# A graph-attention layer with residual and row norm on one core: two blocks leave the table of x rows, and three small pieces of work change places

## The chip, the cores and the metric

The kernel runs on one core of a Trainium2 chip. Its time is device time in microseconds (us). Before the change it takes 233.98 us, the median of three runs (233.9 to 234.27). The profile is of one execution of its own, which took 233.53 us; its span, from the first to the last instruction of the program, is 232.0 us, and the times inside it are counted from its start. The granted TensorE clock is 0.98 of full speed over that execution.

## The reference, cut to what matters

```python
def _L0_gnn_ref(h, adj_mat, W, a):          # h: 4096 x 512, adj: 4096 x 4096, W: 512 x (4*512)
    ht = (h @ W).reshape(N, 4, 512).transpose(1, 0, 2)
    src = jnp.einsum('hnd,hd->hn', ht, a[:, :512, 0])
    dst = jnp.einsum('hnd,hd->hn', ht, a[:, 512:, 0])
    e = jax.nn.leaky_relu(src[:, :, None] + dst[:, None, :], 0.01) + adj_mat[None]
    att = jax.nn.softmax(e, axis=-1)
    return jnp.einsum('hij,hjd->hid', att, ht).mean(axis=0)

x = _layernorm(x + _L0_gnn_ref(x, adj, W, a), axis=-1)
```

The entries of `adj` reach 1e9, and the largest of a row stands far above the second. The softmax then is 1 at that column and 0 elsewhere, so a row of the result is the row of x at the column of the row's maximum, times the mean of W over the heads, plus the row's own x, normalised. The kernel computes that for all rows, tests on the chip that the largest entry leads by enough (with a bound from the norms of x, W and a), and has a general path for inputs where it does not; with these inputs that path is not taken.

## The kernel before, in words

The 4096 rows are worked in 32 blocks of 128 rows, one row on each partition. One Python loop over steps t = 0 to 31 writes the instructions out, in the order in which each engine will run them; nothing is reordered later. A block passes through several steps, so that in one step different engines work on different blocks:

- SP issues the load of block t + 5 of adj (`load_adj`, L128; 2 MB; six buffers) and of x in groups. The general order on its queue is that of the loop; the stores come last.
- VectorE takes maxima over segments of block t (`segment_maxima`, L212), finds the segment with the largest (`find_segment`, L222 and L224), and, two blocks later, the place inside it (`find_column`, L264 and L270). The last block is searched over its whole row (`find_column_in_row`, L278).
- GpSimd gathers the segment that has the maximum (the leads, L230) and then the rows of x at the columns found (`gather_rows`, L250 or L255), with one indirect DMA each for 128 rows.
- TensorE turns the gathered rows of block t - 3 (`turn`: four transposes, L284), adds the block's own x by a product with the identity (`residual`, L296) and multiplies by the mean of W (`products`, L303, four times). ScalarE copies the turned rows (L286), sums squares (L347), and takes mean and variance (L372, L374).
- Blocks from 24 on (`BEHIND`) are handled differently: 24 to 27 are put by (`put_by`, L353), get their x added on GpSimd, and are normalised at the end (`stats`, `late_factors`, `finish`, L366, L368, L391); 28 to 30 get their moments on VectorE (L411, L415), a root on ScalarE (L417), and the normalisation on VectorE (L427). Block 31 is worked in two halves of its columns (L400, L434, L440).

**The table.** `TABLED` lists blocks in which columns below 128 are not gathered. The product of the first 128 rows of x with the mean of W stands in three bf16 parts z. For such a block GpSimd moves those columns out of bounds, so that the gather skips them, ScalarE clears the buffer beforehand (`clear_rows`, L245), `spread` (L331, L333, L335) makes a 0/1 matrix of the columns below 128 and `from_table` (L343) multiplies it with the three parts. In a block that is not in the list the gather fetches all 128 rows; there is no clearing, no spread and no product with z.

**Norms of heads.** `head_norms` has three parts, one a step: `each` on VectorE (L473) and two small products on TensorE (L475, L476); sums on VectorE (L480, L484) and a root on ScalarE (L485); the sum and maximum on VectorE (L488, L489). The result is used only at the end, in `bound` (L507).

Of the kernel before, what the change touches and what calls it, by code (L numbers as in the profile page):

```python
# [26 lines left out]
EARLY = 18  # L27
LAST = 4
SKIP = 8192
TABLED = range(1, 28)  # L30


@with_exitstack
# [40 lines left out]
def leading_rows(ctx, tc, x, adj, W, a, out, ident, leads, any_bad):  # L74
# [11 lines left out]
    KB, NB = D // P, N // P  # L86
# [4 lines left out]
    LATE = NB - Q  # L91
# [200 lines left out]
    def residual(ib):  # L292
        start = ib not in o_ps
        if start:
            o_ps[ib] = psum.tile([P, D], F32, name="o")
        nc.tensor.matmul(o_ps[ib], ident, hold[:, ib, :], start=start, stop=False)  # L296
# [172 lines left out]
    def head_norms(part):  # L469

        if part == 0:
            each = once.tile([2 * H, 2 * H], F32, name="each")
            nc.vector.tensor_scalar_mul(each, ident[: 2 * H, : 2 * H], aa)  # L473
            pw = of_norms[0] = psum.tile([P, KB * H + 2 * H], F32, name="o")
            nc.tensor.matmul(pw[:, : KB * H], ones, ww, start=True, stop=True)  # L475
            nc.tensor.matmul(pw[:, KB * H :], ones[: 2 * H, :], each, start=True, stop=True)  # L476
        elif part == 1:
            pw = of_norms[0]
            w2 = once.tile([P, H], F32, name="w2")
            nc.vector.tensor_reduce(  # L480
                w2, pw[:, : KB * H].rearrange("p (k h) -> p h k", h=H), axis=AX.X, op=OP.add
            )
            for s in range(2):
                nc.vector.tensor_mul(n2[:, ts(s, H)], pw[:, ds(KB * H + s * H, H)], w2)  # L484
            nc.scalar.activation(n2, n2, AF.Sqrt)  # L485
        else:
            both = once.tile([P, H], F32, name="both")
            nc.vector.tensor_add(both, n2[:, :H], n2[:, H:])  # L488
            nc.vector.tensor_reduce(vn, both, axis=AX.X, op=OP.max)  # L489
# [56 lines left out]
    for t in range(NB):  # L546
        if t == NB // 2:
            tc.mark_branch_hint_location("general", engines=HINTED)
        if t in x_at:
            load_x(*x_at[t])  # L550
        if t + AHEAD == NB - 1:
            load_x(LATE, 2)
        load_adj(t + AHEAD)
        middle = PIECES if t in END else 1 if t == NB - 1 else 2
        segment_maxima(t, 0, middle)
        if t >= COLUMN and t not in END and t != COLUMN + 1:
            find_column(t - COLUMN)
            if t == lag_of(BEHIND) + 1:
                scales(slice(BEHIND - 2, BEHIND))
        if t not in END:  # L560
            segment_maxima(t, middle, PIECES)
        if t == NB - 1:
            for ib in (BEHIND, LATE + 2, BEHIND + 2):
                load_x(ib, 2)
        find_segment(t)
        if t in END:
            find_column(t - 1 if t <= COLUMN else t - COLUMN)
        if t + 1 in TABLED:
            clear_rows(t + 1)
        for lo, hi in FACTORS:  # L570
            if t == lag_of(hi):
                nc.vector.reciprocal(sd[:, lo:hi], sd[:, lo:hi])
                if hi < BEHIND:
                    scales(slice(lo, hi))
        if t < 2:
            mean_of_heads(t)
        elif t == 2:
            mean_of_heads(2)
            mean_of_heads(3)
            fill_table()  # L580
        if t == 0:
            square_sums_of_a()
        if 21 <= t < 24:
            head_norms(t - 21)
        ib = t - PROJECT
        if t == NB - 2:
            finish(BEHIND - 3)
            finish(BEHIND - 2)
        if t == NB - 1:
            row_norm(LATE)  # L590
            row_norm(LATE + 1)
            finish(BEHIND - 1)
            residual(LATE + 1)
        if ib >= 0:
            if ib in TABLED:
                spread(ib)
            turn(ib)
            if ib > BEHIND:
                products(ib - 1, KB - 1, KB)
            if ib < BEHIND:  # L600
                residual(ib)
            if ib in TABLED:
                from_table(ib)
            products(ib, 0, KB if ib < BEHIND else KB - 1)
            if ib == 0:
                split_table()
        for _ in range(squares_at.get(t, 0)):
            square_sum_of_w(squares.pop(0))
        if t >= BEHIND + STATS:
            put_by(t - STATS)  # L610
        elif t >= STATS:
            row_norm(t - STATS)
            parked_stats(t - STATS)
        for lo, hi in FACTORS:
            if t == hi - 1 + STATS:
                root(slice(lo, hi))
        for done in FINISHED.get(t, ()):
            finish(done)
# [51 lines left out]
    products_of_half(NB - 1, 0)  # L670
    products_of_half(NB - 1, 1)
    add_sums(NB - 2, hold[:, NB - 2, :])
    moments(NB - 2)
    finish(BEHIND + 2)
    stats_of_half(NB - 1, 0)
    factor(NB - 2)
    normalise(NB - 2, o_ps.pop(NB - 2))
    finish(LATE - 1)
    stats_of_half(NB - 1, 1)
    moments(NB - 1)  # L680
    factor(NB - 1, shift=True)
# [190 lines left out]
```

## Time and profile before

| what | value |
|---|---|
| median of three runs | 233.98 us (233.9 to 234.27) |
| the profiled execution | 233.53 us, span 232.0 us |
| adj loads | 38 issues, 28 of them 2 MB each, landing in a median of 33.1 us |
| gathers of rows of x | 32, median 8.3 us from issue to landing |
| HBM traffic | 418 GB/s over the span |

A row of the page's groups reads: line, engine, operation, what it writes and reads, its count, then the busy time, the mean of one in ns, and the idle time just before it with what ended that. A row of a timeline reads: start in us, duration in us, engine, line, operation, and in square brackets how long the engine was idle before it and what released it. A row of the chain of waits reads: start, duration, what. Matmuls overlap, so in the chain a row of TensorE shows its share of the engine's time and in a timeline its own length.

### The profile page before, as it was taken

The numbers are of one execution on the slowest core, as the hardware profiler recorded it, in microseconds if no ns is written. First come the engines' busy times: TensorE is split into PE (matmuls) and PEld (weight loads), VectorE is DVE, ScalarE is ACT, GpSimd is POOL, SyncE is SP. The second block draws the span as 40 slices with busy tenths as digits, with TensorE's granted clock in tenths as the row PEclk, the third lists the DMA queues.
The fourth block names the chain that finished last, engine by engine and source line by source line (L and its number), as shares of the span: only waits on it lengthen the run. The fifth ranks groups of instructions, "written<-read, shape, count | busy, mean of one in ns | idle before, by whom it ended". The sixth has DMA issues, their size and how long they took to land.

```text
span 232.0 us, 2532 instructions
## 1 busy us (share of the span) xinstructions
PE 197.6 (85%) x604; PEld 95.5 (41%) x614; DVE 189.6 (82%) x296; ACT 153.2 (66%) x378; POOL 111.5 (48%) x254
## 2 busy tenths in 40 slices
PE   0069988779099999997999899999999999999990
PEld 0033443334044444443444345454544444545460
DVE  0448289899879997999699959996999999967882
ACT  3003213588075987797998678878888877958872
POOL 4020414525554556355635665554565665637620
PEclk9999999999859999999999999999999999999997
DMA  6999999999999999999999999999999999999995
GB/s 221 426 435 428 433 421 437 425 431 411 440 429 422 420 437 427 429 421 434 418 433 430 417 435 429 419 430 431 426 432 415 419 425 416 419 416 419 420 374 207
DMA packets 13379, 96.04 MB, mean 414 GB/s; under 512 B 2148, under 2 KB 2596, under 8 KB 7984
## 3 DMA queue, kind: packets, MB, share of 16 engines
q1 hardware_dynamic: 9792, 88.08, 90.0%
q0 software_dynamic: 3552, 7.73, 8.5%
q8 instruction: 6, 0.10, 0.2%
q14 instruction: 13, 0.11, 0.1%
q10 hardware_dynamic: 16, 0.02, 0.0%
HBM read 88.51 MB, written 8.39 MB: 418 GB/s over the span
## 4 chain that ended last, share of the span: by engine, by line
DMA 44%; PE 30%; DVE 19%; ACT 2%; issue 1%; POOL 1%; DVEq 0%; POOLq 0%; ACTq 0%
DMA adj_t<-in_adj_dram 39%; PE o L303 19%; DVE seg L212 15%; DMA y<-in_x_dram,col 4%; PE o L296 3%; PE o L343 3%; PE tp L284 3%; PE o L400 2%; DVE at L224 1%; DVE top L222 1%; DMA a_rows<-in_L_gnn_a_dram 1%; DVE inner L264 1%; POOL lead L230 0%; PE o L396 0%; ACT sq L368 0%
## 5 line engine op out<-in xcount | busy, mean ns | idle before, releaser
L212 DVE TENSOR_REDUCE seg<-adj_t 128x128 f32<-128x2048 f32 (+4 forms) x54 | 138.9, 2589 | 27.4 <-DMA adj_t<-in_adj_dram 27.4
L303 PE MATMUL o<-w_sum,yt 128*128 128x512 f32 x248 | 113.5, 598 | 1.1 <-ACT yt L286 0.8
L303 PEld LDWEIGHTS o<-w_sum,yt 128*128 128x128 f32 x248 | 46.8, 192 | 49.0 <-issue 42.0
L230 POOL DMA_INDIRECT lead<-in_adj_dram,row x31 | 32.5, 1050 | 14.5 <-POOL row L226 14.5
L255 POOL DMA_INDIRECT y<-in_x_dram,col x27 | 29.1, 1077 | 12.1 <-POOL col L272 6.1
L226 POOL TENSOR_TENSOR row<-at,first 128x1 uint32<-128x1 uint32 x31 | 5.8, 188 | 60.0 <-DVE at L224 43.6
L284 PE MATMUL tp<-ident,y 128*128 128x128 f32 x128 | 22.9, 302 | 12.0 <-DMA y<-in_x_dram,col 11.9
L286 ACT COPY yt<-tp 128x512 f32<-128x512 f32 x33 | 19.0, 576 | 14.2 <-PE tp L284 13.9
L451 PE MATMUL o<-hold,ident 128*128 128x512 f32 x32 | 16.4, 671 | 14.0 <-DMA hold<-in_L_gnn_W_dram 14.0
L284 PEld LDWEIGHTS tp<-ident,y 128*128 128x128 f32 x128 | 18.3, 210 | 23.9 <-issue 17.8
L296 PE MATMUL o<-hold,ident 128*128 128x512 f32 x50 | 26.5, 612 | 0.0
L333 ACT ACTIVATE off<-px,minus 128x128 f32<-128x128 f32 x27 | 9.9, 366 | 19.9 <-PE px L331 19.8
L343 PE MATMUL o<-z,pick 128*128 128x512 bf16 x72 | 20.4, 386 | 1.1 <-ACT pick L335 0.8
L347 ACT ACTIVATE sq<-hold 128x512 f32<-128x512 f32 x32 | 20.0, 625 | 0.0
L391 ACT ACTIVATE hold<-hold,nm,sd 128x512 f32<-128x512 f32 x24 | 18.8, 801 | 0.0
L374 ACT ACTIVATE sq<-hold,nm 128x512 f32<-128x512 f32 x24 | 17.3, 722 | 0.8
L452 ACT ACTIVATE w_sum<-o 128x512 f32<-128x512 f32 x4 | 2.4, 597 | 22.5 <-PE o L451 22.5
L245 ACT COPY y<-zero 128x512 f32<-128x512 f32 x27 | 16.3, 603 | 0.0
L451 PEld LDWEIGHTS o<-hold,ident 128*128 128x128 f32 x32 | 6.7, 216 | 22.9 <-issue 21.6
L343 PEld LDWEIGHTS <-pick 128*128 128x128 bf16 x81 | 7.8, 100 | 19.9 <-issue 10.5
L372 ACT ACTIVATE hold<-o 128x512 f32<-128x512 f32 x24 | 14.3, 597 | 0.8
L222 DVE MAX8 top<-seg 128x8 f32<-128x256 f32 (+2 forms) x31 | 11.3, 366 | 1.1
(117 smaller groups left out, 190.3 us busy)
## 6 DMA issues: line engine op xcount, KB each, us to landing
adj_t<-in_adj_dram SPq DMA_DIRECT2D x28, 2048.0 KB, 33.1
adj_t<-in_adj_dram SPq DMA_DIRECT2D x6, 1024.0 KB, 27.3
out_dram<-hold SPq DMA_DIRECT2D x12, 512.0 KB, 10.1
hold<-in_x_dram SPq DMA_DIRECT2D x5, 1024.0 KB, 33.0
hold<-in_L_gnn_W_dram SPq DMA_DIRECT2D x2, 2048.0 KB, 16.5
hold<-in_x_dram SPq DMA_DIRECT2D x4, 512.0 KB, 12.7
adj_t<-in_adj_dram SPq DMA_DIRECT2D x4, 512.0 KB, 18.6
out_dram<-hold SPq DMA_DIRECT2D x4, 256.0 KB, 2.8
```

Of the source, the lines that this page charges most:

```text
L212: nc.vector.tensor_reduce(seg_of[ib][:, ts(k, N // e // n)], adj_t[ib][:, ts(k, N // n)].rearrange("p (s e) -> p s e", e=e), axis=AX.X, op ...
L230: nc.gpsimd.indirect_dma_start(out=lead, out_offset=None, in_=adj_segs[e], in_offset=bass.IndirectOffsetOnAxis(ap=row[:, :1], axis=0),)
L255: nc.gpsimd.indirect_dma_start(out=y_t[ib], out_offset=None, in_=x, in_offset=bass.IndirectOffsetOnAxis(ap=col[:, :1], axis=0), bounds_che ...
L284: nc.tensor.transpose(tp[:, kb, :], y[:, ds(kb, P, KB)], ident)
L286: nc.scalar.copy(yt, tp)
L296: nc.tensor.matmul(o_ps[ib], ident, hold[:, ib, :], start=start, stop=False)
L303: nc.tensor.matmul(o_ps[ib], yt_of[ib][:, kb, :], w_sum[:, kb, :], start=(start and kb == 0), stop=(kb == KB - 1),)
L343: nc.tensor.matmul(o_ps[ib], pick, z[k], start=(start and k == 0), stop=False)
L347: nc.scalar.activation(sq, hold[:, ib, :], AF.Square, accum_out=xx[:, ib : ib + 1])
L374: nc.scalar.activation(sq, hold[:, ib, :], AF.Square, bias=nm[:, i], scale=-float(D), accum_out=sd[:, i])
L391: nc.scalar.activation(hold[:, ib, :], o, AF.Identity, bias=nm[:, i], scale=sd[:, i])
L451: nc.tensor.matmul(o, ident, hold[:, w_at + kb * H + h, :], start=(h == 0), stop=(h == H - 1))
```

## The change

Four edits. Blocks 18 and 19 leave `TABLED`. The three parts of `head_norms` run in steps 16 to 18 instead of 21 to 23. In the last step `residual(29)` stands behind `products(28, 0, 3)` instead of ahead of block 28's turn. In the tail `finish(26)` and `finish(27)` stand ahead of `moments(30)`, whose last instruction is the root of block 30.

```diff
@@ -27,7 +27,7 @@
-TABLED = range(1, 28)
+TABLED = (*range(1, 18), *range(20, 28))
@@ -580,8 +580,8 @@
-        if 21 <= t < 24:
-            head_norms(t - 21)
+        if 16 <= t < 19:
+            head_norms(t - 16)
@@ -590,7 +590,6 @@
             row_norm(LATE)
             row_norm(LATE + 1)
             finish(BEHIND - 1)
-            residual(LATE + 1)
         if ib >= 0:
@@ -604,6 +603,8 @@
             products(ib, 0, KB if ib < BEHIND else KB - 1)
             if ib == 0:
                 split_table()
+        if t == NB - 1:
+            residual(LATE + 1)
@@ -670,12 +671,12 @@
     add_sums(NB - 2, hold[:, NB - 2, :])
+    finish(BEHIND + 2)
+    finish(LATE - 1)
     moments(NB - 2)
-    finish(BEHIND + 2)
     stats_of_half(NB - 1, 0)
     factor(NB - 2)
     normalise(NB - 2, o_ps.pop(NB - 2))
-    finish(LATE - 1)
     stats_of_half(NB - 1, 1)
```

VectorE in step 23, before and then after the change; `seg` holds the segments' maxima, and the number behind a name is that of a buffer:

```order
L222 MAX top<-seg_1428 128x8
L224 MAX_INDEX at<-top,seg_1428 128x8
L488 TENSOR_TENSOR both<-n_156 128x4
L489 TENSOR_REDUCE vn<-both 128x1
L212 TENSOR_REDUCE seg_1489<-adj_t 128x64
```

```order
L222 MAX top<-seg_1399 128x8
L224 MAX_INDEX at<-top,seg_1399 128x8
L212 TENSOR_REDUCE seg_1457<-adj_t 128x64
L264 MAX inner<-lead_1366 128x8
L270 MAX_INDEX within<-top,lead_1366 128x8
```

The two operations of the third part no longer stand between the search in step 23 and the first half of step 24's adj; they now follow the reciprocal of step 18.

TensorE at the end of the loop, in step 31, as a piece of the difference: ahead of it stand the three products of block 27.

```order
 L303 MATMUL o<-w_sum,yt 128x512 x3
-L296 MATMUL o<-hold,ident 128x512
-L284 MATMUL tp<-ident,y 128x128 x4
-L303 MATMUL o<-w_sum,yt 128x512 x5
+L284 MATMUL tp<-ident,y 128x128 x4
+L303 MATMUL o<-w_sum,yt 128x512 x4
+L296 MATMUL o<-hold,ident 128x512
```

Block 28's turn follows block 27's products directly, and block 29's residual stands between the third and the fourth product of block 28.

ScalarE in the tail, from the copy of block 31's turned rows to the last normalisation, as a piece of the difference:

```order
 L286 COPY yt<-tp 128x512
 L417 ACTIVATE sd<-mv,eps 128x1
-L391 ACTIVATE hold<-adj_t,nm,sd 128x512
-L417 ACTIVATE sd<-mv,eps 128x1
-L391 ACTIVATE hold<-adj_t,nm,sd 128x512 x2
-L417 ACTIVATE sd<-mv,eps 128x1
+L391 ACTIVATE hold<-adj_t,nm,sd 128x512 x3
+L417 ACTIVATE sd<-mv,eps 128x1 x2
 L440 ACTIVATE hold<-o,nm,sd 128x256
```

The three normalisations of blocks 25, 26 and 27 now follow one another, and the roots of blocks 30 and 31 come behind them.

## The prediction

> **What bounds the kernel now.** I read the page first (shares, queues), then the chain of waits, then the timeline of single stretches, then the landing of single transfers.
>
> The page's busy row and its two rows on the queues; q1 carries SP's loads and stores, q0 GpSimd's gathers:
>
> ```profile
> PE 197.6 (85%) x604; PEld 95.5 (41%) x614; DVE 189.6 (82%) x296; ACT 153.2 (66%) x378; POOL 111.5 (48%) x254
> q1 hardware_dynamic: 9792, 88.08, 90.0%
> q0 software_dynamic: 3552, 7.73, 8.5%
> ```
>
> Three resources are near full at once: TensorE 85%, VectorE 82%, and the DMA engines 90 + 8.5%. An average does not tell which one ends last, so I went to the chain. It is carried by the table blocks on TensorE from 148.9 us; these are its rows for the two products of step 21 and for block 19, step 22:
>
> ```profile
> 154.57 0.13 PE o L475 x2
> 154.70 0.31 PE o L476 x2
> 160.65 0.06 PE px L331
> 160.70 0.54 PE tp L284 x4
> 161.24 0.86 PE o L296 x2
> 162.10 0.65 PE o L343 x3
> 162.75 3.43 PE o L303 x8
> ```
>
> A table block is 0.06 + 0.54 + 0.86 + 0.65 + 3.43 = 5.54 us with no gap, so by the chain every TensorE instruction counts. But the chain follows one releaser. The timeline of VectorE from 158.53 us on shows a second line beside it:
>
> ```profile
> 158.53 2.29 DVE L212 TENSOR_REDUCE seg<-adj_t 128x64 f32<-128x2048 f32 x1 [2.00 <-DMA adj_t<-in_adj_dram]
> 163.91 0.14 DVE L488 TENSOR_TENSOR both<-n 128x4 f32<-128x4 f32 x1
> 164.16 2.28 DVE L212 TENSOR_REDUCE seg<-adj_t 128x64 f32<-128x2048 f32 x1
> 208.46 0.09 DVE L270 MATCH_VALUE_LOAD within<-top,lead 128x8 f32 x1 [1.83 <-DMA lead<-in_adj_dram,row]
> 208.77 4.42 DVE L278 FIND_INDEX8 col<-top,adj_t 128x8 uint32<-128x4096 f32 x1
> ```
>
> After the 2.00 us stall at 158.53 VectorE has no more idle time until it waits for block 30's leads (208.46). Its search of block 31 (L278, to 213.19) releases the last gather of rows of x. How that gather meets TensorE and ScalarE at the end (landings from the view of the gathers of one short stretch each, below the gather they belong to):
>
> ```profile
> L250 POOL DMA_INDIRECT y<-in_x_dram,col x1: 969/969/969, 209.6 to 209.6; - x1
> DMA to landing us min/median/max: 6.9/6.9/6.9
> L250 POOL DMA_INDIRECT y<-in_x_dram,col x1: 969/969/969, 213.9 to 213.9; - x1
> DMA to landing us min/median/max: 7.2/7.2/7.2
> 212.13 0.63 PE L284 MATMUL tp<-ident,y 128*128 128x128 f32 x4
> 212.80 0.59 ACT L286 COPY yt<-tp 128x512 f32<-128x512 f32 x1 [0.94 <-PE tp L284]
> 216.63 0.75 PE L284 MATMUL tp<-ident,y 128*128 128x128 f32 x4
> 219.92 0.29 ACT L417 ACTIVATE sd<-mv,eps 128x1 f32<-128x1 f32 x1 [0.45 <-DVE mv L415]
> 221.28 0.72 PE L284 MATMUL tp<-ident,y 128*128 128x128 f32 x4 [0.26 <-DMA y<-in_x_dram,col]
> 221.59 0.80 ACT L391 ACTIVATE hold<-adj_t,nm,sd 128x512 f32<-128x512 f32 x1
> 222.29 0.56 ACT L286 COPY yt<-tp 128x512 f32<-128x512 f32 x1
> ```
>
> Block 30's gather lands at 209.56 + 6.9 = 216.45, and its transposes start at 216.63: 0.18 us later. Block 31's lands at 213.95 + 7.2 = 221.15, and its transposes start at 221.28 with TensorE already idle for 0.26 us. **So at the end TensorE is not the bound; the line adj, VectorE, leads, gather is.** One thing of the compute line still counts: block 31's transposes are copied at 222.29, 1.01 us after they began, while block 29's, with ScalarE idle (0.94 us), were copied 0.67 us after theirs began (212.13). ScalarE was still in `finish(24)` (221.59). This gate costs 1.01 - 0.67 = 0.34 us.
>
> **The change part by part.**
>
> (a) *Blocks 18 and 19 out of the table.* TensorE loses the spread and the three products with z, twice: 2 x (0.06 + 0.65) = 1.42 us. ScalarE loses the clearing, `off` and `pick`, GpSimd `low` and a longer start: worth nothing here, since TensorE's five us of work on a block covers theirs. The gathers now fetch all rows. Bytes of q0: leads take 18 x 128 x 64 + 10 x 128 x 128 + 3 x 128 x 256 = 0.41 MB, so rows of x take 7.32 MB = 3575 rows of 2 KB instead of 32 x 128 = 4096; 521 are skipped over 27 blocks, 19 per block. Counted in the inputs, blocks 18 and 19 skip 20 and 27: 47 rows more, 96 KB. By q0's row 8.5% of 232 us over 3552 packets is 5.6 ns a packet with all 16 engines busy: 47 x 5.6 = 0.26 us of DMA, all before the arrival that ended the stall at 158.53. Bounds: nothing (if slots were free) and 47/109 of a whole gather's landing of 8.3 us = 3.6 us; I take 0.26, since queues at 98.5% leave no free slots, and the untabled gathers of blocks 30 and 31 (6.9, 7.2 us) land sooner than the median of all 32, 27 of them tabled:
>
> ```profile
> y<-in_x_dram,col POOLq DMA_INDIRECT x32, 8.3
> ```
>
> How far TensorE can come forward at all shows at block 28, whose turn stands behind block 29's residual (206.42):
>
> ```profile
> L250 POOL DMA_INDIRECT y<-in_x_dram,col x1: 962/962/962, 199.7 to 199.7; - x1
> DMA to landing us min/median/max: 6.1/6.1/6.1
> 206.42 1.02 PE L296 MATMUL o<-hold,ident 128*128 128x512 f32 x2
> ```
>
> Block 28's rows land at 199.7 + 6.1 = 205.8. TensorE is through with block 27 at 206.42 now and can gain 0.6 us there, whatever it saves before.
>
> (b) *Norms of heads to steps 16 to 18.* TensorE loses 0.13 + 0.31 = 0.44 us behind block 17; the pair goes ahead of block 13's spread, where it costs at worst the same 0.44. VectorE: L488 and L489 leave step 23, where they hold it from 163.91 to the next reduce at 164.16: 0.25 us off VectorE's gapless stretch. In steps 16 to 18 all six operations delay VectorE by some 0.8 us (an estimate: three times the 0.25 of two). What hides it is the wait for the adj of step 20:
>
> ```profile
> 139.07 2.29 DVE L212 TENSOR_REDUCE seg<-adj_t 128x64 f32<-128x2048 f32 x1 [2.51 <-DMA adj_t<-in_adj_dram]
> ```
>
> Without that cover it would cost 0.8 us. What is late next is block 17's gather, by up to 0.8 us, and so TensorE at 149; that eats 0.8 of the 1.86 us that (a) and (b) save, and leaves 1.06, still more than the 0.6 that block 28's landing lets through.
>
> How much of the 0.25 us stays on VectorE? Block 24's adj:
>
> ```profile
> L128 SPq DMA_DIRECT2D adj_t<-in_adj_dram x1: 327/327/327, 130.2 to 130.2; - x1
> DMA to landing us min/median/max: 33.8/33.8/33.8
> ```
>
> 130.16 + 33.8 = 163.96, used at 164.16. Without the pair VectorE could start at 163.98: 0.18 us gained at most. With arrivals 0.26 us later it starts at 164.24: 0.08 us lost. **Term: +0.1 us on VectorE, leads and gathers up to the landing of block 31's rows; from -0.18 upward.**
>
> (c) *29's residual behind 28's products.* Same instructions in another order between two turns that stay; 0.86 us (the L296 row) goes from ahead of block 28's turn to behind its third product. It lets block 28's copy, and so ScalarE, start earlier; block 29's turn waits for the same sum. Cost nothing: TensorE does the rest of block 28 meanwhile.
>
> Together, block 29's turn comes some 0.5 us earlier: the 0.6 us at block 28, less the 0.1 us by which its rows land later. Through block 29's products, the bound and VectorE's moments this brings the root at 219.92 to about 219.55, `finish(24)` to 221.2, its end to 222.02. Block 31's turn starts at 221.28 + 0.1 and its copy 0.67 us later, 222.05, against 222.29. **Term: -0.34 + 0.1 = -0.24 us for the start of block 31's products.** Bounds: 0 if ScalarE is still held, -0.34 with no delay of the gather.
>
> (d) *26 and 27 normalised ahead of 30's root.* ScalarE:
>
> ```profile
> 225.03 0.29 ACT L417 ACTIVATE sd<-mv,eps 128x1 f32<-128x1 f32 x1 [1.28 <-DVE mv L415]
> 225.23 1.50 ACT L391 ACTIVATE hold<-adj_t,nm,sd 128x512 f32<-128x512 f32 x2
> 226.66 0.43 DVE L434 BATCH_NORM_STATS2 halves_st<-o 128x6 f32<-128x256 f32 x1 [0.56 <-PE o L400]
> L446 SPq DMA_DIRECT2D out_dram<-hold x1: 332/332/332, 226.8 to 226.8; - x1
> DMA to landing us min/median/max: 2.7/2.7/2.7
> L446 SPq DMA_DIRECT2D out_dram<-hold x1: 333/333/333, 228.7 to 228.7; - x1
> DMA to landing us min/median/max: 2.3/2.3/2.3
> ```
>
> The two finishes fill the 1.28 us in which ScalarE waited, and end near 225 instead of 226.73. Queued behind them is 30's root, then VectorE's normalisation of 30 and the last statistics (226.66), where VectorE had 0.56 us of slack: a root later by up to 0.2 us costs nothing. The store of 26 and 27 starts 1.5 to 1.9 us earlier, so the last store (228.7, landing 2.3 us) finds less ahead of it. The store of 26 and 27 (226.8), twice as large, took 2.7 us; at (88.08 + 7.73) MB / 232 us = 0.41 MB per us a half of it, 0.26 MB, is 0.63 us less, 2.0 to 2.1 us. Bounds: 0 and -0.3 us; I take **-0.12**, since the last store's own data can hardly have waited longer than for the end of block 30's.
>
> The Trainium skill, "DMA: Bandwidth & Descriptors", section "Anatomy of one DMA", gives a transfer a fixed 2.0 us and its bytes at 436 GB/s: an estimate by that page of 2.6 us for this store alone. The row has 2.3 us, already less; by that rule an empty queue would bring nothing, and the sum would be 0.24 us off instead of 0.36.
>
> **Sum:** -0.24 - 0.12 = -0.36 us. The profiled execution has a span of 232.0 us and took 233.53 us; the sum makes 231.6 and 233.17. The median shown is 233.98, 0.45 above the profiled one, so for a median I predict 233.98 - 0.36 = 233.6 us.
>
> **The rivals.**
>
> *Everything falls early.* The 47 rows cost nothing on the adj stream, VectorE keeps its 0.18 us, the gate opens whole, the last store runs free: -0.18 - 0.34 - 0.3 = -0.82, 233.2 us. For it: the DMA share is a mean over slices. Against: VectorE starts within 0.2 us of each adj from block 24 on.
>
> *TensorE's saving reaches the end* as the chain of waits suggests: 1.86 us less, 232.1 us. Against it stand the landings of blocks 28, 30 and 31, which TensorE cannot pass. I give it 2% and count it with the case before.
>
> *Nothing moves.* ScalarE is held as before (30's copy waits for rows that land no earlier, and two blocks' statistics follow it), the store gains nothing: 234.0 us.
>
> *The arrivals slip.* The place is the adj stream of blocks 24 to 27: if the two full gathers hold it longer than their packets' share, VectorE, leads and the last gather follow one to one, with no slack to take it. It turns the sign for the measurement once arrivals slip by 0.16 + 0.34 + 0.12 + 0.47 = 1.1 us, 23 ns a row. Midway between 0.26 and the 3.6 us of the bound, 1.9 us, the time is 233.98 + 1.9 - 0.16 - 0.46 = 235.3 us. Against it: the landings of the untabled gathers above.
>
> **How the numbers follow.** A measurement of this kernel tells 0.2%, 0.47 us, from no change: below 233.51 counts as faster, above 234.45 as slower. Likeliest, 0.52: the sum, 233.6 with 0.2 us to either side; the edge 233.51 lies inside, and 0.20 of it falls below. Early, 0.24, faster. Nothing moves, 0.12, same. Arrivals slip, 0.12, slower. Faster 0.20 + 0.24 = 0.44, same 0.32 + 0.12 = 0.44, slower 0.12. The range 233.0 to 234.1 holds the first three, less the 2% and a little at the upper edge, and leaves out the last.
>
> **What would show it.** In the changed profile: no L343 for blocks 18 and 19, and TensorE idle ahead of the turns of blocks 28, 30 and 31, ended by the gather (right) or still gapless (then TensorE was the bound). Block 31's transposes at 221.3 to 221.5, copied 0.67 us later without `finish(24)` in between. Block 24's reduce at 164.2; at 165 or later the arrivals slipped. The store of 26 and 27 issued before 225.3 and the last store landing in 2.0 to 2.3 us. I am wrong if block 31's transposes move by more than 0.3 us either way, or if the end of its products does not follow them.

## The result, and the profile after

The change makes the kernel slower. Its median is 234.49 us (234.12 to 235.06) against 233.91 us (233.47 to 234.35) for the kernel before, timed beside it; the ratio is 1.0024, 95% interval 1.0017 to 1.0031, or +0.56 us (0.40 to 0.73). 233.6 was predicted, a gain.

The profiled executions are 1.30 us apart (234.83 and 233.53 us, spans 233.2 and 232.0), more than the medians: the one before lies 0.4 us under its median, the one after 0.3 us over. So up to 0.7 us of any shift between these two profiles can be chance; a shift is a finding only where several kernels repeat it.

The busy rows and the queues of the page after:

```profile
PE 197.0 (84%) x597; PEld 94.7 (41%) x606; DVE 189.7 (81%) x296; ACT 151.4 (65%) x372; POOL 110.1 (47%) x250
q1 hardware_dynamic: 9792, 88.08, 89.6%
q0 software_dynamic: 3552, 7.83, 8.6%
```

The edits did what they say: TensorE's count falls from 604 to 597, and q0 carries 0.10 MB more, the 47 rows. VectorE's timeline after, at the wait of step 20, the stall, block 24 and the last search:

```profile
139.00 2.29 DVE L212 TENSOR_REDUCE seg<-adj_t 128x64 f32<-128x2048 f32 x1 [1.56 <-DMA adj_t<-in_adj_dram]
159.03 2.29 DVE L212 TENSOR_REDUCE seg<-adj_t 128x64 f32<-128x2048 f32 x1 [2.74 <-DMA adj_t<-in_adj_dram]
164.42 2.29 DVE L212 TENSOR_REDUCE seg<-adj_t 128x64 f32<-128x2048 f32 x1
209.35 4.42 DVE L278 FIND_INDEX8 col<-top,adj_t 128x8 uint32<-128x4096 f32 x1
```

The norms vanish in the wait of step 20, as said: it shrinks from 2.51 to 1.56 us and ends at the same time. The stall of step 23 ends at 159.03 (before 158.53), block 24's reduce starts at 164.42 (before 164.16), the last search 0.58 us later.

On TensorE, the timeline before shows the transposes of blocks 26 and 28,

```profile
197.13 0.70 PE L284 MATMUL tp<-ident,y 128*128 128x128 f32 x4
207.28 0.63 PE L284 MATMUL tp<-ident,y 128*128 128x128 f32 x4
```

and the view of the gathers' line the issue and landing of block 26's rows:

```profile
L255 POOL DMA_INDIRECT y<-in_x_dram,col x1: 1087/1087/1087, 189.5 to 189.5; - x1
DMA to landing us min/median/max: 6.7/6.7/6.7
```

The timeline after, with the transposes of blocks 26, 28, 29 and 31 and the copy of 31:

```profile
197.58 0.72 PE L284 MATMUL tp<-ident,y 128*128 128x128 f32 x4 [0.83 <-DMA y<-in_x_dram,col]
206.90 0.63 PE L284 MATMUL tp<-ident,y 128*128 128x128 f32 x4
212.60 0.63 PE L284 MATMUL tp<-ident,y 128*128 128x128 f32 x4
221.88 0.72 PE L284 MATMUL tp<-ident,y 128*128 128x128 f32 x4 [0.39 <-DMA y<-in_x_dram,col]
222.75 0.56 ACT L286 COPY yt<-tp 128x512 f32<-128x512 f32 x1
```

The gather of block 26 after, in the view of its line:

```profile
L255 POOL DMA_INDIRECT y<-in_x_dram,col x1: 1089/1089/1089, 190.0 to 190.0; - x1
DMA to landing us min/median/max: 7.5/7.5/7.5
```

TensorE stands idle for 0.83 us at block 26, and there its saving ends: the rows land at 190.0 + 7.5 = 197.5 instead of 189.5 + 6.7 = 196.2, some 1.2 us later. Other profiles repeat the wait: in all seven kernels with blocks 18 and 19 out of the table TensorE waits there, for 0.50 to 0.83 us, and in none of the eleven others. It takes up block 26 at 196.88 to 197.61 in the seven and at 197.13 to 197.72 in the eleven, in the mean 0.2 us earlier. Block 31's transposes start 0.60 us later than before (221.88 against 221.28), twice what the prediction allowed.

The tail after, from its timeline (225.65 is the issue of the store of 26 and 27):

```profile
225.53 0.28 ACT L417 ACTIVATE sd<-mv,eps 128x1 f32<-128x1 f32 x1
225.65 3.82 SPq L446 DMA_DIRECT2D out_dram<-hold  x3
227.13 0.43 DVE L434 BATCH_NORM_STATS2 halves_st<-o 128x6 f32<-128x256 f32 x1 [0.54 <-PE o L400]
228.56 0.56 ACT L440 ACTIVATE hold<-o,nm,sd 128x256 f32<-128x256 f32 x1 [0.42 <-DVE nm L422]
```

The stores of block 30 and of block 31 after, from views of their line over a short stretch each:

```profile
L446 SPq DMA_DIRECT2D out_dram<-hold x1: 332/332/332, 226.6 to 226.6; - x1
DMA to landing us min/median/max: 4.3/4.3/4.3
L446 SPq DMA_DIRECT2D out_dram<-hold x1: 332/332/332, 229.1 to 229.1; - x1
```

The whole tail lies 0.46 us later than before (block 31's products start at 223.37 against 222.91), and measured from there the root of block 30 is not late (225.53 against 225.03). VectorE still waits 0.54 us for TensorE ahead of the last statistics, and ScalarE has no wait ahead of the root any more: on the engines the tail is as predicted. The stores are not. From the issue of the last store to the end of the span it takes 233.2 - 229.15 = 4.0 us, before 232.0 - 228.68 = 3.3 us. That is 0.7 us more, about the whole loss in the medians. Where it lies is seen in the DMA share of three stretches (last two columns: share of 16 engines, GB/s), before

```profile
228.50:229.50 1.00, 0.00 (x0) 0.00 (x0) 0.01 (x1) 0.16 (x1) 0.00 (x0) 1.00 0.99 389
231.00:231.50 0.50, 0.00 (x0) 0.00 (x0) 0.00 (x0) 0.00 (x0) 0.00 (x0) 0.50 0.00 0
231.50:232.00 0.50, 0.00 (x0) 0.00 (x0) 0.00 (x0) 0.00 (x0) 0.00 (x0) 0.50 0.00 0
```

and after:

```profile
228.50:229.50 1.00, 0.00 (x0) 0.00 (x0) 0.48 (x2) 0.56 (x1) 0.00 (x0) 0.90 0.32 125
231.00:231.50 0.50, 0.00 (x0) 0.00 (x0) 0.00 (x0) 0.00 (x0) 0.00 (x0) 0.50 0.12 41
231.50:232.00 0.50, 0.00 (x0) 0.00 (x0) 0.00 (x0) 0.00 (x0) 0.00 (x0) 0.50 0.03 12
```

Before, the engines are full up to the last store and idle behind 231. After, they have almost run dry when the last store is issued, and from 231.0 on 0.12 x 16 = 1.9 engines' worth of packets is still under way: some 14 engines are through, two are not.

### The profile page after: what moved, and what is told of

Same layout as the page of the kernel before. It is cut to its first block, busy times and chain, and to the rows that moved or that the text cites. A ratio compares the mean times of both kernels' runs of the same rounds, so it can differ in the third digit from the quotient of the medians.

```text
span 233.2 us, 2502 instructions
## 1 busy us (share of the span) xinstructions
PE 197.0 (84%) x597; PEld 94.7 (41%) x606; DVE 189.7 (81%) x296; ACT 151.4 (65%) x372; POOL 110.1 (47%) x250
## 4 chain that ended last, share of the span: by engine, by line
DMA 53%; DVE 23%; PE 9%; POOL 7%; issue 5%; ACT 1%; POOLq 0%; DVEq 0%; ACTq 0%
DMA adj_t<-in_adj_dram 39%; DVE seg L212 17%; DMA y<-in_x_dram,col 7%; DMA lead<-in_adj_dram,row 6%; PE o L303 5%; POOL lead L230 2%; DVE at L224 2%; PE o L400 2%; POOL y L255 1%; DVE col L278 1%; DVE top L222 1%; PE o L296 1%; PE tp L284 1%; DMA a_rows<-in_L_gnn_a_dram 1%; DVE within L270 1%
## 5 line engine op out<-in xcount | busy, mean ns | idle before, releaser
L255 POOL DMA_INDIRECT y<-in_x_dram,col x25 | 26.8, 1071 | 10.3 <-POOL col L272 6.4
L333 ACT ACTIVATE off<-px,minus 128x128 f32<-128x128 f32 x25 | 9.1, 365 | 18.6 <-PE px L331 18.5
L343 PE MATMUL o<-z,pick 128*128 128x512 bf16 x67 | 19.0, 387 | 0.9 <-ACT pick L335 0.6
L245 ACT COPY y<-zero 128x512 f32<-128x512 f32 x25 | 15.1, 603 | 0.0
L343 PEld LDWEIGHTS <-pick 128*128 128x128 bf16 x75 | 7.2, 100 | 18.6 <-issue 10.8
```

Source lines behind the costliest of these rows:

```text
L255: nc.gpsimd.indirect_dma_start(out=y_t[ib], out_offset=None, in_=x, in_offset=bass.IndirectOffsetOnAxis(ap=col[:, :1], axis=0), bounds_che ...
L343: nc.tensor.matmul(o_ps[ib], pick, z[k], start=(start and k == 0), stop=False)
```

## The experiments

Each kernel was timed against the kernel before on the same chip (its medians there 233.9 to 234.1 us); a ratio has its 95% interval.

### Which part of the change costs the time

The first theory was that the gathers of the full blocks slip, the second that the tail does.

The table edit alone:

```diff
-TABLED = range(1, 28)
+TABLED = (*range(1, 18), *range(20, 28))
```

> Blocks 18 and 19 out of the table, nothing else of the change. Theory 1 (the 47 more rows of x hold up the adj stream, and VectorE, the leads and the last gathers follow): the adj of step 23 lets VectorE start at 158.9 to 159.1 us instead of 158.53, the last row gather lands some 0.5 to 0.8 us later, the time is 0.4 to 0.8 us over the kernel before. It should be no better than the whole change, since the 0.24 us of the norms stay on VectorE. Theory 2 (the tail's new order costs the time): no difference, within 0.2 us. Theory 3 (the norms in steps 16 to 18 cost it): within 0.2 us or faster.

Measured: 233.90 us, ratio 0.9998 (0.9981 to 1.0015). The first theory falls.

The norms of heads alone:

```diff
-        if 21 <= t < 24:
-            head_norms(t - 21)
+        if 16 <= t < 19:
+            head_norms(t - 16)
```

> Norms of heads in steps 16 to 18, nothing else. Theory 1: VectorE takes the adj of step 24 up to 0.18 us earlier, the 0.8 us that steps 16 to 18 lose vanish in the wait of step 20; time -0.2 to 0 us. Theory 3: VectorE's delay of 0.8 us in steps 16 to 18 is handed on through later buffers and gathers; +0.3 to +0.8 us. Theory 2: within 0.2 us.

Measured: 233.91 us, ratio 0.9993 (0.9982 to 1.0003).

The tail alone, that is the residual and the two finishes:

```diff
-            residual(LATE + 1)
...
+        if t == NB - 1:
+            residual(LATE + 1)
...
-    moments(NB - 2)
     finish(BEHIND + 2)
+    finish(LATE - 1)
+    moments(NB - 2)
...
-    finish(LATE - 1)
```

> 29's residual behind 28's products and 26, 27 normalised ahead of 30's root, nothing else. Theory 2 (the store of 26 and 27 that starts earlier runs into the last stores, or the root is late): +0.3 to +0.6 us, with the last store landing 2.8 us or more after its issue. Theory 1: -0.2 to +0.1 us, root of 30 at 225.0 to 225.3 and the start of block 31's products as before.

Measured: 234.58 us, ratio 1.0022 (1.0011 to 1.0032): the loss of the whole change.

The whole change without the table edit (the two diffs above):

> The norms, the residual and the order of the tail, with blocks 18 and 19 kept in the table. Theory 1: VectorE's stall at step 23 ends at 158.5 as before, time 0.1 to 0.4 us under the kernel before. Theory 2 or 3: still 0.3 us or more over it.

Measured: 234.74 us, ratio 1.0026 (1.0014 to 1.0037). So the table edit neither makes the loss nor hides a larger one.

The tail in its two halves: the residual alone,

> Block 29's residual behind block 28's products, nothing else of the change. Theory of the stores (the time is lost because the store of blocks 26 and 27 is issued earlier and the last stores then overlap): no earlier store here, so 0 within 0.2 us, stores of 26 and 27, 30 and 31 issued within 0.2 us of 226.8, 227.2 and 228.7, the last landing in 2.3 to 2.8 us. Rival, the residual: VectorE's sum or TensorE's two products are late behind block 28's and cost the tail +0.5 us by themselves.

measured 234.04 us, ratio 1.0002 (0.9993 to 1.0010), and the two finishes alone,

> Blocks 26 and 27 normalised ahead of 30's root, nothing else of the change. Theory of the stores: the store of 26 and 27 issued near 225.6, the last store issued within 0.2 us of 228.7 but landing in about 3.1 us; +0.4 to +0.6 us. Rival, the order on ScalarE: 30's root and the last statistics are late and the last store is issued 0.4 us later. Rival, the residual (then the loss is not here): 0 within 0.2 us.

measured 234.86 us, ratio 1.0032 (1.0022 to 1.0043), the last store issued at 229.0 and landing in 3.3 us. And all of the change but the finishes:

> The whole change but for its last part: blocks 26 and 27 are normalised where they were before. Theory of the stores: the loss is gone, and what is left is worth nothing that can be measured, so within 0.2 us of the kernel before; the last store lands in 2.3 to 2.8 us. Rival (the table edit and the norms together delay block 26's gather): +0.4 us or more. By the terms of the prediction it would be 0.24 us faster.

Measured: 233.84 us, ratio 1.0004 (0.9992 to 1.0015). **The loss is in the finishes of 26 and 27**, and the other three edits together are worth nothing that the medians can tell. Its single times are not quite those of the kernel before, though: four of its twelve executions took 234.44 us or more, and none of the 18 of the kernel before on that chip.

### Is it the order on ScalarE or the store

The finishes stay early, but SP issues the store of 26 and 27 behind that of block 30:

```diff
-    for ib, n in ((LATE, 2), (BEHIND, 2), (BEHIND + 2, 2), (NB - 2, 1)):
+    for ib, n in ((LATE, 2), (BEHIND, 2), (NB - 2, 1), (BEHIND + 2, 2)):
```

> The finishes of 26 and 27 early as before this, but on SP the store of 26 and 27 is issued behind the store of block 30, so not before block 30 is normalised. Theory of the stores: with the early store gone its cost goes too; the last store lands in 2.3 to 2.8 us and the time is within 0.2 us of the kernel before. If the overlap alone (three stores within 2.5 us) costs, and not the earliness, the stores of 30, then 26 and 27, then 31 lie even closer, and the last lands in 2.8 us or more: +0.3 us. Rival, the order on ScalarE: +0.5 us whatever the stores do.

Measured: 234.11 us, ratio 1.0002 (0.9994 to 1.0011). The engines' work is that of the kernel at 1.0032; only the order of two stores differs. So **the early store costs the time, not the early finishes**.

The same in the whole change:

> The whole change, but on SP the store of 26 and 27 is issued behind that of block 30. Theory of the stores: 0.5 us less than the whole change, so from 0.2 us faster than the kernel before to the same. Rival (the change loses its time ahead of the stores, at block 26's gather): stays at +0.5 us.

Measured: 234.19 us, ratio 1.0013 (1.0000 to 1.0026), 0.1% below the whole change, less than expected but in its direction. The two intervals overlap, so this run alone would not show it; the pair before does.

### Why a store that goes earlier makes the last one later

My words for it so far were that the last stores overlap. The rival came from the packets' records: all engines run dry, and then two 8 KB packets of queue 14 (kind: instruction) come in amid the last store. Views of the DMA queues over short stretches show them; in the kernel before, from 229.2 to 230.4, then from 230.4 to 230.6 (packets, MB, share of 16 engines),

```profile
q1 hardware_dynamic: 220, 0.39, 84.5%
...
q14 instruction: 2, 0.02, 20.3%
q1 hardware_dynamic: 1, 0.00, 0.2%
```

and in the kernel after, from 230.1 to 230.3, then from 231 to 233:

```profile
q1 hardware_dynamic: 34, 0.07, 89.0%
q14 instruction: 2, 0.02, 39.5%
...
q1 hardware_dynamic: 16, 0.03, 3.8%
```

Before, the two packets come when the store's data are through (one packet of q1 is left). After, they come amid it, and 16 of its packets follow from 231 on.

To tell the two apart, the kernel before without the two middle stores:

```diff
-    for ib, n in ((LATE, 2), (BEHIND, 2), (BEHIND + 2, 2), (NB - 2, 1)):
+    for ib, n in ((LATE, 2), (BEHIND, 2)):
```

> The kernel before with the stores of blocks 26, 27 and 30 left out (their rows of the output are not written), so that the last store finds empty queues. Theory of the overlap (it is the stores ahead that make the last one late): the last store lands in 2.0 to 2.3 us, and the time is 0.2 to 0.5 us below the kernel before. Rival, the instruction packets (two 8 KB packets of queue 14 come about 1.06 us after the last store's issue and hold two of the DMA engines for 0.6 to 0.8 us, unless the stores ahead still fill the queues): with nothing ahead the two packets fall amid the last store, which lands in 2.8 to 3.1 us, and the time is 0.3 to 0.6 us above the kernel before, though it stores less.

Measured: 234.94 us, ratio 1.0039 (1.0024 to 1.0054): it writes 0.75 MB less and is 0.9 us slower. The overlap falls: there is nothing left to overlap. Its last store, in the view of the stores' line:

```profile
L446 SPq DMA_DIRECT2D out_dram<-hold x1: 333/333/333, 228.8 to 228.8; - x1
DMA to landing us min/median/max: 3.4/3.4/3.4
```

Its DMA queues from 229.0 to 230.6, and from 230.6 to 232.2:

```profile
DMA packets 128, 0.25 MB, mean 154 GB/s; under 512 B 14, under 2 KB 14, under 8 KB 126
q1 hardware_dynamic: 126, 0.23, 37.1%
q14 instruction: 2, 0.02, 2.6%
...
DMA packets 18, 0.03 MB, mean 20 GB/s; under 512 B 2, under 2 KB 2, under 8 KB 18
q1 hardware_dynamic: 18, 0.03, 8.5%
```

The store is 128 x 2 KB, eight packets for each of 16 engines, and one short packet more for each at the end. Up to 230.6, 126 - 14 = 112 of them have gone, all of 14 engines, and 14 short ones; behind the two instruction packets come 16 and 2 short ones, **the whole share of two engines**. The same records also speak against the packets' own length as the whole reason. The view from 229.8 to 230.3 has no packet of queue 14 yet:

```profile
q1 hardware_dynamic: 87, 0.18, 91.3%
```

An engine that works on the store starts a packet every 80 ns, six and a quarter in half a microsecond; 87 are those of 14 engines. The 14 start on the store at 229.67 to 229.77, the two instruction packets only at 230.35 and 230.36, for 0.31 and 0.35 us, and the first packet of the two late engines starts at 230.66. So these two had carried nothing for over half a microsecond before the instruction packets came; what held them is not shown.

The change's finishes with the store of block 30 left out (the diff of the finishes, and `(NB - 2, 1)` out of the list):

> Blocks 26 and 27 normalised ahead of 30's root, as in the change, and the store of block 30 left out (its rows of the output are not written). Theory of the overlap: only the store of 26 and 27, issued 3.4 us ahead, is still before the last one, which lands in 2.0 to 2.4 us; the time is the kernel before's or less. Rival, the instruction packets: the queues are as empty as can be, the last store still lands in 2.8 to 3.1 us, and the time stays 0.5 us or more above.

Measured: 234.72 us, ratio 1.0033 (1.0020 to 1.0045), landing in 3.3 us. Again the queues are dry and the store late.

The kernel before with only block 30's store left out:

> The kernel before with the store of block 30 left out (its rows of the output are not written), all else in place. Theory of the dry queues: the store of 26 and 27, issued at 226.8, ends near 229.0; the DMA share from 228.5 to 229.5 falls from 1.0 to about 0.5; the last store finds a gap of some 0.7 us and lands later, 2.6 to 3.3 us, time 0.1 to 0.4 % above the kernel before though it writes less. Theory of the overlap: lands in 2.0 to 2.3 us, time the same or less.

Measured: 233.90 us, ratio 0.9991 (0.9982 to 1.0001). That was a miss for the dry queues as I had put it: the DMA share did fall, to 0.59 between 228.5 and 229.5, and nothing became late. What this kernel still has is data under way at the moment when ScalarE ends its program. The stretch from 0.2 us before to 0.3 us after that end shows it in the column before the last, the DMA share. The kernel before:

```profile
228.46:228.96 0.50, 0.00 (x0) 0.00 (x0) 0.05 (x1) 0.20 (x1) 0.00 (x0) 1.00 0.97 389
```

The kernel after:

```profile
228.92:229.42 0.50, 0.00 (x0) 0.00 (x0) 0.06 (x1) 0.20 (x1) 0.00 (x0) 0.88 0.30 119
```

Without the two middle stores:

```profile
228.60:229.10 0.50, 0.00 (x0) 0.00 (x0) 0.06 (x1) 0.20 (x1) 0.00 (x0) 0.85 0.00 0
```

Without the store of block 30 alone:

```profile
228.70:229.20 0.50, 0.00 (x0) 0.00 (x0) 0.05 (x1) 0.20 (x1) 0.00 (x0) 1.00 0.75 303
```

So the third form of the theory: what counts is whether the engines still carry store packets when ScalarE ends and, 0.02 us later, the last store is issued. The kernel before with only the store of 26 and 27 left out should then be as fast as before:

> The kernel before with the store of 26 and 27 left out (their rows of the output are not written) and that of block 30 kept. Against the kernel without both stores it writes one store of 0.25 MB more, issued near 227.2, whose packets run from 228.2 to 228.9. Theory of the moment (what counts is whether the DMA engines still carry store packets when ScalarE ends its program and the last store is issued; if not, the two instruction packets go first on two engines): they do here, at least in part, so the last packet ends 1.7 to 2.3 us after the issue, and the time is 0.5 to 1.0 us below the kernel without both stores, that is at the kernel before within 0.2 us, although it writes more. Theory of the stores ahead (whatever their moment): the time of the kernel without both, 0.9 us above the kernel before, or later.

Measured: 234.88 us, ratio 1.0035 (1.0023 to 1.0047). The expected time was wrong, and the reason is on SP: with no store of 26 and 27 in front, that of block 30 no longer waits and is issued at 226.2, not at 227.2, and none of its packets starts after 228.5. The share at ScalarE's end is 0.00, and by the theory's own condition the store has to be late: from 230.8 to 231.3 the share is 0.10, 1.6 engines. The run agrees with the condition, not with my reading of the order.

### Filling the gap

If dry engines are the trouble, other data in their place should cure it. In the whole change, the store of 24 and 25 put behind 30's:

```diff
-    for ib, n in ((LATE, 2), (BEHIND, 2), (BEHIND + 2, 2), (NB - 2, 1)):
+    for ib, n in ((LATE, 2), (BEHIND + 2, 2), (NB - 2, 1), (BEHIND, 2)):
```

> The whole change, early finishes and all, but on SP the store of blocks 24 and 25 is issued last before the final one, behind those of 26, 27 and of 30. Nothing is computed otherwise; the same bytes go out, 0.5 MB of them later. Theory of the empty queues (the last store is late because the queues have run dry when it comes, and the two 8 KB instruction packets then go ahead of two engines' share of it): 1.3 MB issued from 225.7 on at 0.41 MB per us fill the engines to about 229.7, as in the kernel before; the two instruction packets fall behind the last store's data, which lands in 2.3 to 2.8 us; 0.4 to 0.6 us less than the whole change, so within 0.2 us of the kernel before. Theory of the overlap (stores close ahead make the last one late): more bytes close ahead, the last store lands in 3.2 us or more, 0.5 to 0.9 us above the kernel before.

Measured: 234.73 us (233.87 to 235.18), ratio 1.0024 (1.0012 to 1.0036). A miss in the time. Two stretches of it, at ScalarE's end and from 2.0 to 2.5 us after the last store's issue:

```profile
229.03:229.53 0.50, 0.00 (x0) 0.00 (x0) 0.05 (x1) 0.20 (x1) 0.00 (x0) 1.00 1.01 401
231.25:231.75 0.50, 0.00 (x0) 0.00 (x0) 0.00 (x0) 0.00 (x0) 0.00 (x0) 0.50 0.05 20
```

The engines are full, but one of them (0.05 x 16 = 0.8) is behind by itself. In the packets' records the last 4 KB packet of 24 and 25's store ends at 231.40, and eight packets of 2 KB, one engine's share of the last store, follow it until 232.05. One instruction packet of 16 KB starts at 228.2 and takes 0.96 us; that it was this engine's is likely and not shown, since the trace does not name DMA engines.

Half of that, only block 25's store late:

```diff
+    for ib, n in ((LATE, 2), (BEHIND, 1), (BEHIND + 2, 2), (NB - 2, 1), (BEHIND + 1, 1)):
```

> The whole change, but of the store of 24 and 25 only block 24 goes early; block 25's 0.25 MB are issued behind block 30's store. Theory of the moment: 1.0 MB from 225.7 on keep the engines busy to about 229.1, where ScalarE ends; the last packet ends 1.7 to 2.3 us after the issue, and the time is 0.3 to 0.6 us below the whole change, at the kernel before within 0.2 us. If a single engine is behind by itself, as with all of 24 and 25 late, one engine alone ends late and the time stays at that of the whole change. Theory of the stores ahead: 0.5 us or more above the kernel before, with all engines late.

Measured: 234.99 us (234.20 to 235.07), ratio 1.0036 (1.0023 to 1.0049). In the profiled execution, which took 234.20 us, the share at ScalarE's end is 1.06 and the last packet ends 2.1 us after the issue, as expected; but the median is 0.8 us above that execution, so what it shows is not what sets the time of this kernel. That stays open.

Block 30's store issued twice in the whole change:

> The whole change, and behind block 30's store the same store once more (the same bytes to the same rows), so 0.25 MB more are written than needed. Theory of the dry queues: the DMA share from 228.5 to 229.5 rises from 0.3 to 0.7 or more, the last store lands in 2.3 to 2.8 us, and the kernel that writes more is 0.3 to 0.5 us faster than the whole change, so at most 0.1 % above the kernel before. Theory of the overlap: the last store lands in 3.2 us or more, and the time is 0.24 % or more above the kernel before.

Measured: 236.13 us, ratio 1.0090 (1.0076 to 1.0103). It decided nothing: the second store was not issued until the first had landed (4.4 us after 226.1), presumably as it writes the same rows, and the last store waited behind it. One thing can be taken from it: here ScalarE's end and the last store are 2.35 us apart, the instruction packets are through at 230.2, and the last packet of the last store ends 1.8 us after its issue, with no engine late. The DMA share is 0.00 from 230.6 to 231.1, so the engines were dry when that store was issued (the second copy of block 30's, 0.4 us ahead of it, had not begun to move). So dry engines alone did not make the last store late here; it is one profile of one kernel.

### The runs side by side

The share is that from 0.2 us before to 0.3 us after ScalarE's last instruction ends; "late" is the DMA share from 2.0 to 2.5 us after the last store's issue, times 16; "last packet" is the time from that issue to the end of its last packet. The ratio is that of the medians; all that stands behind it is read from one profiled execution of each kernel, whose own time is in the last column.

| kernel | ratio | share | late engines | last packet, us | profiled, us |
|---|---|---|---|---|---|
| before | 1 | 0.97 | 0 | 1.7 | 233.53 |
| without 30's store | 0.9991 | 0.75 | 0 | 1.7 | 233.90 |
| residual alone | 1.0002 | 0.96 | 0 | 1.7 | 233.73 |
| norms alone | 0.9993 | 0.96 | 0 | 1.7 | 234.02 |
| change without finishes | 1.0004 | 0.99 | 0 | 2.0 | 233.72 |
| change, store behind 30's | 1.0013 | 1.02 | 0.5 | 2.3 | 233.64 |
| table alone | 0.9998 | 0.78 | 0.6 | 2.4 | 234.18 |
| finishes, store behind 30's | 1.0002 | 0.80 | 1.6 | 2.7 | 234.56 |
| the change | 1.0024 | 0.30 | 1.8 | 2.6 | 234.83 |
| tail alone | 1.0022 | 0.25 | 1.1 | 2.6 | 234.68 |
| all but the table | 1.0026 | 0.22 | 1.8 | 2.7 | 234.94 |
| finishes alone | 1.0032 | 0.23 | 1.8 | 2.9 | 234.92 |
| finishes, no store of 30 | 1.0033 | 0.06 | 2.1 | 2.9 | 234.72 |
| no store of 26 and 27 | 1.0035 | 0.00 | 1.6 | 2.5 | 234.29 |
| no middle stores | 1.0039 | 0.00 | 1.8 | 2.9 | 234.94 |
| change, 24 and 25's store late | 1.0024 | 1.01 | 0.8 | 2.8 | 235.06 |
| change, 25's store late | 1.0036 | 1.06 | 0.2 | 2.1 | 234.20 |

Every kernel with a share of 0.30 or less is slower than before by 0.2% or more. Of those with 0.75 or more, all but the two that put 24's or 25's store late are within 0.13%. Two kernels look odd by their medians: the finishes with the store behind 30's (late engines, yet 1.0002) and the change with 25's store late (hardly a late engine, yet 1.0036). By the time of the profiled execution itself they fall in line. The six executions whose last packet ends within 2.1 us took 233.53 to 234.20 us, the three at 2.3 to 2.5 us 233.64 to 234.29, and the eight at 2.6 us or more 234.56 to 235.06.

Single executions of a kernel spread as widely as that: with 24 and 25's store late, three of twelve took 233.87 to 233.96 us and the others 234.42 to 235.18. It may be that the late engines come in some executions of a kernel and not in others, and that the median tells how often. One profile of each kernel can't show that.

## Why the prediction was wrong

**(a) and the bound, half right.** That TensorE's saving does not reach the end was right. The price of the 47 rows, 0.26 us on the arrivals, can't be read from the time of the table edit alone (0.9998, or -0.44 to +0.35 us). In the profiles the stall of step 23 ends at 158.62 to 159.03 in the seven kernels with that edit and at 158.21 to 158.53 in the eleven without, 0.4 us apart in the mean: dearer than 0.26, and far from the 1.9 us of the rival. Wrong was the place where TensorE is stopped. I took block 28, with room for 0.6 us; it is block 26. Its rows landed 0.9 us before their use (196.2 against 197.13), and in the changed kernel they land 1.2 us later. The step that failed is "that eats 0.8 of the 1.86 us that (a) and (b) save, and leaves 1.06, still more than the 0.6 that block 28's landing lets through": it looked at the landing of one late block only and took the gathers between as unmoved.

The prediction's bold sentence, that at the end the line of adj, VectorE, leads and gather is the bound and TensorE is not, failed as well, by its own 0.34 us: block 31's copy waited for ScalarE, and ScalarE for what TensorE had done from block 26 on. From block 26's turn to block 31's copy it takes 25.16 us before (197.13 to 222.29) and 25.17 after (197.58 to 222.75), and 25.15 to 25.19 in 16 of the 18 profiles, whether block 31's rows come early or late. In the two others, 25.23 and 25.38, they came later still. With the store behind 30's, the whole change has block 31's transposes 0.56 us earlier than before (220.72), and the copy comes only 0.23 us earlier, as block 26's turn does (196.88 against 197.13):

```profile
220.72 0.75 PE L284 MATMUL tp<-ident,y 128*128 128x128 f32 x4
222.06 0.56 ACT L286 COPY yt<-tp 128x512 f32<-128x512 f32 x1
```

**(b) right in its parts.** The wait of step 20 took the norms in; block 24's reduce came at 164.42, between the 164.2 that I expected and the 165 that I named as the sign of slipping arrivals.

**The gate on ScalarE, -0.24: wrong, it measured nothing.** It rested on block 29's turn coming 0.5 us earlier: "the 0.6 us at block 28, less the 0.1 us by which its rows land later". Those 0.6 us never came. In the change without the finishes, where the gate should show undisturbed, TensorE is through with block 27 at 206.50, against 206.42 before, since it had waited for block 26. Block 28's transposes come 0.78 us earlier (206.50 against 207.28) only because 29's residual, 0.86 us, no longer stands ahead of them; it stands behind them now, and block 29's come at 212.20, against 212.13 before. That (c) by itself moves block 28 and not block 29 was as predicted. Block 31's copy follows its transposes by 222.36 - 221.41 = 0.95 us, not 0.67. The timeline of that kernel, transposes of 28, 29 and 31 and the copy of 31:

```profile
206.50 0.63 PE L284 MATMUL tp<-ident,y 128*128 128x128 f32 x4
212.20 0.63 PE L284 MATMUL tp<-ident,y 128*128 128x128 f32 x4
221.41 0.72 PE L284 MATMUL tp<-ident,y 128*128 128x128 f32 x4 [0.32 <-DMA y<-in_x_dram,col]
222.36 0.56 ACT L286 COPY yt<-tp 128x512 f32<-128x512 f32 x1
```

In time, these three edits make a ratio of 1.0004 (0.9992 to 1.0015), +0.09 us (-0.19 to +0.35), where the terms gave -0.24.

**(d) The store, -0.12: wrong in sign, and this decided the case.** ScalarE and VectorE did what the step says, the root of 30 was not late, and the store went out 1.1 us earlier (225.65 against 226.76; I had said before 225.3; in the tail that lies 0.46 us later that is 1.6 us). What failed is "finds less ahead of it", taken as a gain. It found less ahead of it and ended later: the finishes alone cost 0.0032 x 233.97 = 0.75 us (0.51 to 1.0). I priced a transfer by bytes ahead of it and bounded the term at 0 to -0.3 us; no bound on the other side was worked out, and no rival had its place in the stores. The data of 14 engines behave as I said: in the kernel without middle stores all their packets are through by 230.46, 1.64 us after the issue, against 1.72 us for all 16 in the kernel before. The transfer, though, landed only with its slowest engine: after 2.3 us where the last packet ended at 1.7, after 3.4 us where it ended at 2.9.

By the Trainium skill, "DMA: Bandwidth & Descriptors", section "Anatomy of one DMA — SWDGE (gpsimd) path", a transfer on GpSimd's path takes a fixed 2.0 us and its bytes at 436 GB/s. Carried over to this store, which SP issues, as the prediction did, that is an estimate of 2.6 us with or without an empty queue, and the store term would be 0. That is nearer than mine, but the same 256 KB landed in 2.3 us in the kernel before and in 3.4 us with nothing ahead of them; neither a fixed price nor bytes ahead gives that spread.

**Shown and not shown.** Shown by runs: the loss comes with the finishes, and goes when the store alone is put back behind 30's. Shown by the records: it lies in one or two DMA engines that are late with the last store, in all seven kernels of the table whose engines had run dry when ScalarE ended, and with two instruction packets right ahead of the late data. Not shown is that these packets are the cause: the trace does not say which engine a packet ran on, the packets could not be taken away, in the kernel without middle stores the two late engines were already empty before the packets came, and the two kernels with a store of 24 or 25 late were slow although their engines were full; late engines also show at shares of 0.78 and 0.80 (0.6 and 1.6 engines). For the packets, or something else at ScalarE's end, speaks the kernel that stores block 30 twice: dry engines, the packets long through, and no engine late. Why the last store is late stays open.

Of the rivals none was this one. "Arrivals slip" had the right sign and the wrong place; its condition, 1.1 us of slip at the last gather, was not met (0.6 us, in one pair of profiles, and 0.1 us in the change without finishes).

## What to carry to other kernels

The store here was over when the slowest of its engines was (it landed 0.4 to 0.6 us after its last packet), so a store at the end of a program isn't priced by its bytes or by what is ahead of it alone: look at how many engines are still at work in its last half microsecond (share times 16). Moving a store out of the way of the last one can cost more than it saves; test it by itself, with the computation moved and the store left in place, as the pair at 1.0032 and 1.0002 does. And a saving on an engine ends at the first wait that it runs into: check the landing of every block on the way, here block 26, before a later gate is credited with it.

## What the hardware showed that was not expected

- Leaving out 0.75 MB of stores ahead of the last one made the kernel 0.9 us slower (1.0039), and the landing of that last store went from 2.3 to 3.4 us.
- Two 8 KB instruction packets run soon after ScalarE has ended its program. The first starts 1.06 to 1.10 us after its last instruction in six of the seven kernels of the table whose engines had run dry (1.55 us in the kernel without middle stores), 1.45 to 1.93 us after it in the ten others.
- In the kernel without middle stores two of the 16 DMA engines began on the last store 0.9 us after the others, with no packet of any kind for the first 0.6 us of that.
- A 16 KB packet of instructions took 0.92 to 1.89 us of a DMA engine near the end of these kernels (0.96 us at 228.2 in the kernel with 24 and 25's store late), as long as eleven or more 2 KB packets of a store at 84 ns each.
